# Later gates in a recurrent layer with a mixture of experts: five pairs of experts further down the program

## The chip, the cores and the metric

The kernel runs on one core of a Trainium2 chip. A core has five engines that run at the same time, each with its own queue of instructions, kept in order: TensorE (PE, matrix products; its weight loads are listed as PEld), VectorE (DVE), ScalarE (ACT), GpSimd (POOL) and SyncE (SP, which here issues the transfers). They wait for one another through semaphores. The metric is the device time of one execution in microseconds (us); lower is better. The kernel before takes 1005.94 us, the median of three runs (1005.19 to 1009.68).

## The reference

The input x has 8 batches of 1024 time steps of 256 features. In short:

```
xn = layernorm(x)
v  = xn Wv^T + bv
for each time step t:            # W starts as W0
    y_t = xn_t W^T               # the output uses W before its update
    W   = W - eta * 2/(B*D) * (y_t - v_t)^T xn_t
logits = xn Wr^T + br            # 16 experts
p      = softmax(logits), the six largest kept and divided by their sum
moe    = sum over experts e of  gate_e * (xn E_e)
out    = x + y * silu(moe)
```

All 16 expert products are computed for every token, and the gates (10 of the 16 are zero) weight them.

## The kernel before

**Tiles and slots.** Tokens go in 64 tiles of 128 rows, 16 time steps of 8 batches each. The main loop gives each tile a slot, and in a slot eight pairs of experts follow one another: `experts(i, pair)` runs six matmuls that fill one PSUM bank h with both experts' products (L539). Of each pair, DVE adds the even expert's part to a running sum (mix, L558), and for six of the odd experts ACT scales (part, L547) and POOL adds (mix, L550); the other two odd ones are DVE's as well. There are three h banks.

**The recurrence.** In its slot, a tile also has three steps that follow from W: errors_1 before pair 0, errors_2 before pair 3, update before pair 5. In errors_1 PE multiplies by W (pe), DVE forms p, and p is split into a high and a low part (p_hi on ACT, p_lo on DVE). In errors_2 PE makes the errors, ACT scales them to step_hi (L510), and DVE makes step_lo (L512) and hy (L516). In update six matmuls add to W in PSUM (wt_ps; the third is the first to use step_lo), and then W is split (wt_hi on ACT, wt_lo on DVE). Every split goes through the helper `split` (L142, L143), and most products through `accumulate` (L241).

**Ahead of W.** Five tiles ahead, other steps are put between the pairs: the load of x and the layer norm (DVE's st, mv and xn, POOL's ve and rstd, then xr, a transpose whose blocks change places by way of DRAM), the transposed tile's split (xT_two, xn_hi, xn_lo), `project` before pair 1 and `project_end` before pair 2. `project` makes the Gram matrix in gram, ACT copies a part of it to cross (L256), and DVE adds the router's bias to the logits lg. In `project_end` one matmul of PE adds cross transposed (L268), and DVE forms xx (L276) and a (L277).

**Groups.** Tiles are grouped: groups 0 to 3 have 1, 1, 2 and 4 tiles, all others (4 to 17) have 4. After a group's last projection come its gates, and, one pair later, `solve_0` (four q additions on DVE, L407); five further solve steps between later pairs invert the group's triangular matrices. The gates of groups 4 to 17 stand in the slots of tiles 6, 10, ... 58. They are DVE's work but for one exponential on ACT:

- the eight largest logits (top), the difference d to the largest, ex on ACT
- four match instructions, which mark the six largest (L366)
- s_all, chosen (L372), s_top (L375), den (L377), r_den (L378), total, acc, eps_sum, acc again, and gate (L382)

chosen, a, q, den and gate each read two tensors from SBUF; mix and xx read one from PSUM and one from SBUF.

**What sets the order.** PE and SP keep the order of the program. The other three engines' instructions are placed by a planner that runs when the program is built: it works with estimated times, takes what is ready, and goes by the program's order among those. So a step's place in the program is a wish for DVE, ACT and POOL, and the order in the built program is fixed.

Of the kernel before, what the change touches and what calls it, by code (L numbers as in the profile page):

```python
"""Layer norm, then an online-learned linear layer (one gradient step of W per time step) gated by
the silu of a top-6-of-16 mixture of linear experts, with a residual.

Tokens go in tiles of 128 rows: 16 time steps of all 8 batches, time-major. Within a tile the
recurrence is solved exactly: with A = c * X X^T restricted to strictly earlier time steps and
c = eta * 2 / (B * D), the errors of all steps are E = T (X W^T - V), T = (I + A)^-1, where W is the
weight before the tile, and W^T is then lowered by c * X^T E. The state W^T accumulates in one PSUM
bank.

U = T^T is built for a few tiles at a time from diagonal blocks of 32 rows, by Horner's rule  # L10
(I - C (I - C (I - C)), C = A^T), which merge into blocks of 64 and then 128 rows:
U_ab = -U_a C_ab U_b.

TensorE and the DMA queue keep the order given below; the other engines are scheduled around them.
All but the first tiles are transposed without TensorE: in blocks of 32 by VectorE, and the blocks
change places on their way through DRAM.

The large products split each float32 operand exactly into two float32r parts, x = hi + lo, and add
up hi*hi + hi*lo + lo*hi in float32; what is left out is below float32's own rounding.
"""  # L20

# [1 line left out]

# [11 lines left out]
PSUM = bass.MemoryType.PSUM  # L35
# [5 lines left out]
EPS = 1e-10  # L41
# [2 lines left out]
GROUP = 4  # L44
AHEAD = 5
BY_PE = 4
ON_ACT = (1, 3, 5, 7, 9, 11)


@with_exitstack  # L50
def ttt_moe_kernel(
# [13 lines left out]
    B, S, D = x.shape  # L65
# [10 lines left out]
    state = ctx.enter_context(tc.tile_pool(name="state", bufs=2))  # L76
# [11 lines left out]
    counts = [1, 1, 2]  # L88
# [22 lines left out]
    def misc(name):  # L111
        return ps_misc.tile([P, 512], F32, tag="misc", name=name)

# [1 line left out]
    raws = {}  # L115

    def fetch_expert(e):
# [19 lines left out]
    make_identity(nc, ident)  # L137
    neg_half = const.tile([P, 1], F32)
    nc.gpsimd.memset(neg_half, -0.5)
    # transposed weights: W0^T the first state, [Wv^T | router^T] one moving operand  # L140
    def split(hi, lo, src, engine=None):
        nc.scalar.copy(hi, src)  # L142
        (engine or nc.vector).tensor_sub(lo, src, hi.bitcast(F32))  # L143
# [37 lines left out]
    def at(b, size=Q):  # L181
        return slice(b * size, (b + 1) * size)

# [1 line left out]
    class Prepared:  # L185
        pass

# [2 lines left out]
    def layernorm(i):  # L190
        q = tiles[i] = Prepared()
        xt = x_tile(i)
        st = small.tile([P, nc.vector.BN_STATS_DIM], F32, tag="st", name=f"st_{i}")
        nc.vector.bn_stats(st, xt)  # L194
        mv = small.tile([P, nc.vector.BN_AGGR_DIM], F32, tag="mv", name=f"mv_{i}")
        nc.vector.bn_aggr(mv, st)  # L196
        ve = small.tile([P, 1], F32, tag="ve", name=f"ve_{i}")
        nc.gpsimd.tensor_scalar_add(ve, mv[:, 1:2], LN_EPS)  # L198
        rstd = small.tile([P, 1], F32, tag="rstd", name=f"rstd_{i}")
        nc.gpsimd.tensor_tensor(rstd, ve, neg_half, ALU.pow)  # L200
        q.xn = work.tile([P, D], F32, tag="xn", name=f"xn_{i}", bufs=3)
        nc.vector.tensor_scalar(q.xn, xt, mv[:, 0:1], rstd, ALU.subtract, ALU.mult)  # L202
        if i < BY_PE:
            return
        q.xT = work.tile([P, KD * P], F32, tag="xT", name=f"xT_{i}", bufs=3)
        # blocks of 32 are transposed in place, and change places by way of DRAM
        xr = work.tile([P, D], F32, tag="xr", name=f"xr_{i}")
        nc.vector.transpose(
            xr.rearrange("p (c k t) -> p k c t", c=NQ, k=KD),
            q.xn.rearrange("p (k c t) -> p k c t", c=NQ, k=KD),  # L210
        )
        bounce = dram.tile([NQ, Q, NQ, KD * Q], F32, tag="bounce", name=f"bounce_{i}")
        nc.sync.dma_start(out=bounce.rearrange("b d c f -> (b d) (c f)"), in_=xr)
        for c in range(NQ):
            nc.sync.dma_start(
                out=q.xT[at(c), :].rearrange("p (b f) -> p b f", b=NQ),
                in_=bounce[:, :, c, :].rearrange("b d f -> d b f"),
            )
# [15 lines left out]
        split(q.xn_hi, q.xn_lo, q.xn, nc.gpsimd)  # L234

    def accumulate(o, hi, lo, rhs_hi, rhs_lo, first=True, **kw):
        # the terms with the moving low part come last: it is ready last
        terms = [t for a, b, r in zip(hi, lo, rhs_hi) for t in ((a, r), (b, r))]
        terms += zip(hi, rhs_lo)
        for m, (a, b) in enumerate(terms):  # L240
            nc.tensor.matmul(  # L241
                o, lhsT=a, rhs=b, start=first and m == 0, stop=(m == len(terms) - 1), **kw
            )

    def project(i, g, j):
        q = tiles[i]
        # X X^T = H H^T + H L^T + (H L^T)^T
        gram = misc(f"gram_{i}")
        for k in range(KD):
            nc.tensor.matmul(  # L250
                gram[:, : 2 * P], lhsT=q.xT_hi[:, k, :],
                rhs=q.xT_two[:, k, :, :].rearrange("p n t -> p (n t)"),
                start=(k == 0), stop=(k == KD - 1), skip_group_check=True,
            )
        q.gram, q.cross = gram, work.tile([P, P], F32R, tag="cross", name=f"cross_{i}")
        nc.scalar.copy(q.cross, gram[:, P : 2 * P])  # L256
        vr = misc(f"vr_{i}")
        accumulate(
            vr[:, :NVR],
            [q.xT_hi[:, k, :] for k in range(KD)], [q.xT_lo[:, k, :] for k in range(KD)],  # L260
            [w_vr[0][:, k, :] for k in range(KD)], [w_vr[1][:, k, :] for k in range(KD)],
        )
        nc.vector.tensor_add(g.lg[:, j, :NE], vr[:, D:NVR], bias[:, D:])  # L263
        q.vr = vr
# [11 lines left out]
        nc.vector.tensor_add(xx, q.gram[:, :P], q.cross.bitcast(F32))  # L276
        nc.vector.tensor_mul(g.a[:, j, :, :], xx.unsqueeze(1).broadcast_to([P, 2, P]), masks)  # L277

# [1 line left out]
    layernorm(0)  # L280
    transpose_w()
    ident_r = const.tile([P, P], F32R)
# [6 lines left out]
    half_b = const.tile([P, D], F32)  # L289
    nc.scalar.mul(half_b, bias[:, :D], 0.5)  # L290

    # -c at strictly earlier time steps, in A's place and in A^T's
    ones = const.tile([P, P], F32)
    nc.gpsimd.memset(ones, 1.0)
    keep = const.tile([P, 2, P], F32)
# [8 lines left out]
    masks = const.tile([P, 2, P], F32)  # L304
    nc.vector.tensor_scalar_mul(masks, keep, neg_c)

    # U and the first half of T by blocks: what is never written stays zero
    u_full, t_half = [], []
    for n in range(2):
        u = const.tile([P, GROUP, P], F32, tag=f"u_{n}", name=f"u_{n}")  # L310
# [8 lines left out]
    def open_group(n, first, count):  # L319
# [14 lines left out]
        for name, t in vars(stores[m]).items():  # L334
            if name in ("t", "z2"):
                setattr(g, name, t)
            else:
                setattr(g, name, t[:, j : j + count])
        # odd tiles keep the first half of T, and what comes of it, in the upper partitions
        g.halves = []  # L340
        for odd in range(2):
            js = [n for n in range(count) if (j + n) % 2 == odd]
# [5 lines left out]
    def gates(g):  # L348
# [5 lines left out]
        def narrow(name):  # L354
            return group.tile([P, GROUP], F32, tag=name, name=f"{name}_{n}", bufs=4)[:, :c]

        # the six largest logits, the first of equal ones, are marked; two absent values fill up to eight
        lg, top, d, ex = g.lg, wide("top", 8), wide("d"), wide("ex")
        marked, chosen, gate = wide("marked", NE + 2), wide("chosen"), wide("gate", bufs=4)
        for j in range(c):  # L360
# [12 lines left out]
            chosen, marked[:, :, :NE], TAKEN, ex, op0=ALU.is_equal, op1=ALU.mult  # L373
        )
        nc.vector.tensor_reduce(s_top, chosen, AX.X, ALU.add)  # L375
        # gates p / (sum p + EPS) with p = ex / s_all, then divided by max(their sum, EPS)
        nc.vector.scalar_tensor_tensor(den, s_all, EPS, s_top, op0=ALU.mult, op1=ALU.add)  # L377
        nc.vector.reciprocal(r_den, den)  # L378
        nc.vector.tensor_mul(total, s_top, r_den)
# [7 lines left out]
            q.u_hi, q.u_lo = g.u_hi[:, j, :], g.u_lo[:, j, :]  # L387

    def step_q(g, name, rhs, out):
        """I - C rhs for the diagonal blocks."""  # L390
        c = g.count
        ps = solving(f"{name}_ps_{g.n}")
        for j in range(c):
            for b in range(P // Q):
                nc.tensor.matmul(  # L395
                    ps[at(b), j * Q : (j + 1) * Q], lhsT=g.a[at(b), j, 0, at(b)],
                    rhs=rhs[at(b), j, :], start=True, stop=True, skip_group_check=True,
                )
        nc.vector.tensor_add(
            out, ps[:, : c * Q].rearrange("p (j q) -> p j q", q=Q),  # L400
            ident_q.unsqueeze(1).broadcast_to([P, c, Q]),
        )
# [81 lines left out]

    solve = [solve_1, solve_2, solve_3, solve_4, solve_5, solve_6]

# [1 line left out]
    def errors_1(i):  # L488
        q = tiles[i]
        q.pe = ps_rec.tile([P, 2 * D], F32, tag="pe", name=f"pe_{i}")  # L490
# [70 lines left out]
                q.mix[j] = new  # L561

    def finish(i):
        # x + y silu(m) = x + (y / 2) m (1 + tanh(m / 2))
        q = tiles[i]
        xt = x_tile(i)
        m = work.tile([P, D], F32, tag="m", name=f"m_{i}")
# [9 lines left out]
            out=out[:, i * TS : (i + 1) * TS, :].rearrange("b t d -> t b d"), in_=o  # L577
        )

# [1 line left out]
    opened = {}  # L581

    def project_x(i):
        n, first, j = where[i]
        if n not in opened:
            opened[n] = open_group(n, first, counts[n])
        project(i, opened[n], j)
        if j == counts[n] - 1:
            gates(opened[n])

    def project_y(i):
        n, first, j = where[i]
# [4 lines left out]
    def solve_x(n, m):  # L597
        solve[m](opened[n])

    # what comes before each (tile, pair of experts)  # L600
    events = {}

    def put(slot, pair, what, *args):
        events.setdefault((slot, pair), []).append((what, args))

    # the first tiles have a schedule of their own: (slot, pair) as 8 * slot + pair
    chain = {
        0: (3, 9, 10), 1: (13, 16, 18), 2: (21, 23, 25), 3: (27, 29, 31), 4: (33, 38, 40),
        5: (42, 45, 47), 6: (49, 51, 55),
# [18 lines left out]
    for i in range(1, NT):  # L628
# [6 lines left out]
        put(turn // 8, turn % 8, transpose_x, i)  # L635
        put(spot // 8, spot % 8, project_x, i)
        put((spot + 1) // 8, (spot + 1) % 8, project_y, i)

    ctx.enter_context(tc.manual_schedule(engines={mybir.EngineType.PE, mybir.EngineType.SP}))

# [52 lines left out]
```

## Time and profile before

| | |
|---|---|
| time, median of three runs | 1005.94 us (1005.19 to 1009.68) |
| span of the profiled execution | 1004.7 us |
| PE busy | 977.6 us, 97% |
| DVE busy | 770.0 us, 77% |
| ACT busy, POOL busy | 436.5 us, 440.8 us |
| granted PE clock | full speed after the first twentieth of the span |
| four tiles in the steady part | 60.3 us |

The span is measured from the first to the last instruction of one execution under the profiler; the runs' times are taken without it. Times in a timeline count from the span's start. A line of the timeline gives start and length, engine, source line, operation, output and inputs, their sizes, how many instructions were merged (x2), and in brackets how long the engine had been idle and what ended that. Buffer numbers are left out of names, so that every running sum is mix and both q buffers are q.

### The profile page before, as it was taken

How to read it: one execution, taken by the hardware profiler on the slowest of the kernel's cores; microseconds unless marked ns; L12 is line 12 of the kernel's file. 1: busy time of each engine (PE TensorE's matmuls, PEld its weight loads, DVE VectorE, ACT ScalarE, POOL GpSimd, SP SyncE). 2: the span in 40 equal slices, each digit the busy share in tenths (PEclk: the TensorE clock that was granted, in tenths of full speed). 3: DMA queues.
4: the chain of work that ended last, by engine and by line, in shares of the span. 5: the costliest groups of instructions: out<-in, count | busy, mean ns of one | idle time of the engine just before them, and what ended most of it. 6: DMA issues, size and time to landing. Idle time of an engine off the chain costs nothing.

```text
span 1004.7 us, 19617 instructions
## 1 busy us (share of the span) xinstructions
PE 977.6 (97%) x6672; PEld 799.9 (80%) x6672; DVE 770.0 (77%) x2225; ACT 436.5 (43%) x1174; POOL 440.8 (44%) x677
## 2 busy tenths in 40 slices
PE   5899999999999999999999999999999999999997
PEld 4677888878888887888878888887888878888785
DVE  7888797777878777787777878778787777867665
ACT  5454444344443534435344443534435344443432
POOL 6544344444344344444444344344444444344333
PEclk8899999999999999999999999999999999999999
DMA  7021111111111111111111111011111111100000
GB/s 231 17 53 49 39 27 43 37 27 43 39 27 42 28 37 43 38 27 44 38 28 43 38 28 43 24 42 43 36 29 43 38 28 43 35 25 11 12 11 11
DMA packets 67092, 38.65 MB, mean 38 GB/s; under 512 B 38176, under 2 KB 66992, under 8 KB 66992
## 3 DMA queue, kind: packets, MB, share of 16 engines
q1 hardware_dynamic: 66992, 37.41, 13.6%
q8 instruction: 52, 0.85, 0.3%
q14 instruction: 48, 0.39, 0.1%
HBM read 21.13 MB, written 16.25 MB: 37 GB/s over the span
## 4 chain that ended last, share of the span: by engine, by line
PE 77%; DVE 14%; issue 2%; POOL 2%; DMA 2%; ACT 2%; SPq 1%; POOLq 0%; DVEq 0%; ACTq 0%
PE h L241 59%; PE pe L241 6%; PE wt_ps L241 4%; PE vr L241 3%; DVE q L407 3%; DVE mix L558 2%; DMA x<-in_L_attn_x_dram 1%; PE gram L250 1%; DVE marked L366 1%; POOL mix L550 1%; DVE st L194 1%; ACT part L547 1%; DVE o L574 1%; DVE d L362 1%; PE uq_ps L395 1%
## 5 line engine op out<-in xcount | busy, mean ns | idle before, releaser
L241 PE MATMUL h<-we,xT_two 128*128 128x512 f32 x3072 | 789.3, 402 | 4.5 <-DVE mix L558 2.5
L241 PEld LDWEIGHTS h<-we,xT_two 128*128 128x128 f32 x3072 | 554.5, 189 | 120.1 <-issue 2.7
L558 DVE SCALAR_TENSOR_TENSOR mix<-h,gate,mix 128x256 f32<-128x256 f32 x576 | 265.6, 475 | 112.0 <-PE h L241 80.1
L547 ACT ACTIVATE part<-h,gate 128x256 f32<-128x256 f32 x384 | 182.1, 474 | 293.1 <-DVE mix L558 171.4
L550 POOL TENSOR_TENSOR mix<-mix,part 128x256 f32<-128x256 f32 x256 | 188.7, 737 | 131.4 <-ACT part L547 124.0
L572 POOL TENSOR_TENSOR my<-m,hy 128x256 f32<-128x256 f32 x64 | 47.3, 739 | 159.0 <-DVE m L568 159.0
L550 POOL TENSOR_TENSOR mix<-part,part 128x256 f32<-128x256 f32 x64 | 47.9, 749 | 72.3 <-ACT part L547 72.3
L575 POOL TENSOR_TENSOR o<-o,x 128x256 f32<-128x256 f32 x63 | 46.5, 738 | 69.4 <-DVE lg L263 59.2
L194 DVE BATCH_NORM_STATS2 st<-x 128x6 f32<-128x256 f32 x64 | 27.1, 425 | 49.9 <-DMA x<-in_L_attn_x_dram 49.5
L241 PE MATMUL vr<-w_vr,xT_two 128*128 128x272 f32 x384 | 59.2, 290 | 0.0
L202 DVE TENSOR_SCALAR xn<-x,mv,rstd 128x256 f32<-128x256 f32 x64 | 49.0, 765 | 12.2 <-POOL rstd L200 11.9
L143 DVE TENSOR_TENSOR wt_lo<-wt_ps,wt_hi 128x512 fp32r<-128x512 f32 x64 | 42.9, 671 | 19.6 <-ACT wt_hi L142 19.5
L142 ACT CAST xT_two<-xT 128x256 fp32r<-128x256 f32 x60 | 24.4, 407 | 71.9 <-PE h L241 69.9
L198 POOL TENSOR_SCALAR ve<-mv 128x1 f32<-128x1 f32 x64 | 14.5, 228 | 91.2 <-DVE mv L196 56.4
L143 POOL TENSOR_TENSOR xn_lo<-xn,xn_hi 128x256 fp32r<-128x256 f32 x64 | 47.7, 746 | 14.2 <-ACT xn_hi L142 13.9
L142 ACT CAST p_hi<-p 128x256 fp32r<-128x256 f32 x64 | 26.0, 406 | 63.6 <-DVE p L498 63.5
L241 PEld LDWEIGHTS vr<-w_vr,xT_two 128*128 128x128 f32 x384 | 52.4, 191 | 0.0
L510 ACT ACTIVATE step_hi<-pe,neg_c 128x256 fp32r<-128x256 f32 x64 | 30.4, 474 | 50.5 <-PE pe L241 50.2
L241 PEld LDWEIGHTS pe<-wt_hi,xT_two 128*128 128x128 f32 x256 | 39.2, 189 | 5.9
L142 ACT CAST wt_hi<-wt_ps 128x512 fp32r<-128x512 f32 x64 | 37.2, 581 | 10.8 <-PE wt_ps L241 10.3
L241 PE MATMUL pe<-wt_hi,xT_two 128*128 128x256 f32 x256 | 40.7, 281 | 0.0
L143 DVE TENSOR_TENSOR p_lo<-p,p_hi 128x256 fp32r<-128x256 f32 x64 | 39.2, 612 | 0.9 <-ACT p_hi L142 0.4
(115 smaller groups left out, 1186.7 us busy)
## 6 DMA issues: line engine op xcount, KB each, us to landing
x<-in_L_attn_x_dram SPq DMA_DIRECT2D x64, 128.0 KB, 2.7
out_dram<-o SPq DMA_DIRECT2D x64, 128.0 KB, 2.3
bounce<-xr SPq DMA_DIRECT2D x60, 128.0 KB, 2.4
xT<-bounce SPq DMA_DIRECT2D x240, 32.0 KB, 1.8
raw<-in_L_ffn_expert_w_dram SPq DMA_DIRECT2D x16, 256.0 KB, 5.0
w_raw<-in_L_attn_Wkv_dram SPq DMA_DIRECT2D x1, 256.0 KB, 3.1
w_raw<-in_L_attn_W_dram SPq DMA_DIRECT2D x1, 256.0 KB, 5.2
bias<-in_L_attn_bkv_dram SPq DMA_DIRECT2D x1, 128.0 KB, 4.5
```

Of the source, the lines that this page charges most:

```text
L142: nc.scalar.copy(hi, src)
L143: (engine or nc.vector).tensor_sub(lo, src, hi.bitcast(F32))
L194: nc.vector.bn_stats(st, xt)
L202: nc.vector.tensor_scalar(q.xn, xt, mv[:, 0:1], rstd, ALU.subtract, ALU.mult)
L241: nc.tensor.matmul(o, lhsT=a, rhs=b, start=first and m == 0, stop=(m == len(terms) - 1), **kw)
L407: nc.vector.tensor_add(g.q1[at(b)], g.a[at(b), :, 1, at(b)], ident_q[at(b), :].unsqueeze(1).broadcast_to([Q, c, Q]),)
L510: nc.scalar.mul(q.step_hi, e, neg_c)
L547: nc.scalar.mul(part, he, gate)
L550: nc.gpsimd.tensor_add(new, q.mix[1], part)
L558: nc.vector.scalar_tensor_tensor(new, he, gate, q.mix[j], op0=ALU.mult, op1=ALU.add)
L572: nc.gpsimd.tensor_mul(my, m, q.hy)
L575: (nc.vector if i == NT - 1 else nc.gpsimd).tensor_add(o, o, xt)
```

## The change

From group 4 on (`LATE_GATES`), the gates are no longer emitted with the projection of the group's last tile, which stands before pair 1, but by an event of their own, five pairs later in the same slot: before pair 6, behind the update of W, which stands before pair 5. The instructions stay as they are. What a group's gates are used for begins with the next group's first slot, two slots later.

```diff
+LATE_GATES = 4
...
     def project_x(i):
         n, first, j = where[i]
         if n not in opened:
             opened[n] = open_group(n, first, counts[n])
         project(i, opened[n], j)
-        if j == counts[n] - 1:
+        if j == counts[n] - 1 and n < LATE_GATES:
             gates(opened[n])
 
+    def gates_x(n):
+        gates(opened[n])
...
         put(spot // 8, spot % 8, project_x, i)
         put((spot + 1) // 8, (spot + 1) % 8, project_y, i)
+        n, first, j = where[i]
+        if n >= LATE_GATES and j == counts[n] - 1:
+            put((spot + 5) // 8, (spot + 5) % 8, gates_x, n)
```

## The prediction

> **What bounds the kernel now.** I read the page's first part, then the chain that ended last, the waits of TensorE (PE), and then the timeline of single tiles.
>
> ```profile
> PE 977.6 (97%) x6672; PEld 799.9 (80%) x6672; DVE 770.0 (77%) x2225; ACT 436.5 (43%) x1174; POOL 440.8 (44%) x677
> ...
> PE 77%; DVE 14%; issue 2%; POOL 2%; DMA 2%; ACT 2%; SPq 1%; POOLq 0%; DVEq 0%; ACTq 0%
> ...
> PE wt_ps L241 <- DVE step_lo L512: 2.4, 9, 0.4
> ```
>
> PE is the bound, busy 97% of the span with an order that is fixed; only what makes PE wait, or wait longer, changes the time. In the steady part four tiles take 60.3 us. One wait recurs, once per group, in the slot (the eight pairs of one tile) where gates stand: PE's update of W waits for step_lo. In the timeline the six update matmuls, from the first to the next product's start, take 0.71 us in 48 of the 63 updates and 1.07 to 1.41 us in 12, those of tiles 10, 14, ... 54; with 0.71 taken off each, the 12 sum to 5.9 us. (Three early ones are longer for other reasons and aren't touched.) So 5.9 us is the most that a perfect cure brings.
>
> The timeline of tile 26 (group 9's gates) shows why:
>
> ```profile
> 438.50 0.48 DVE L558 SCALAR_TENSOR_TENSOR mix<-h,gate,mix 128x256 f32<-128x256 f32 x1
> 439.22 0.22 DVE L372 SCALAR_TENSOR_TENSOR chosen<-marked,ex 128x64 f32<-128x64 f32 x1
> 439.35 0.42 DVE L277 TENSOR_TENSOR a<-xx,masks 128x256 f32<-128x256 f32 x1
> 439.69 0.74 POOL L550 TENSOR_TENSOR mix<-part,part 128x256 f32<-128x256 f32 x1 [0.94 <-ACT part L547]
> 439.81 0.48 DVE L558 SCALAR_TENSOR_TENSOR mix<-h,gate,mix 128x256 f32<-128x256 f32 x1
> 440.20 0.66 DVE L407 TENSOR_TENSOR q<-a,ident_q 32x128 f32<-32x128 f32 x2
> 441.00 0.74 POOL L550 TENSOR_TENSOR mix<-mix,part 128x256 f32<-128x256 f32 x1 [0.57 <-ACT part L547]
> 441.09 1.09 DVE L407 TENSOR_TENSOR q<-a,ident_q 32x128 f32<-32x128 f32 x2
> 442.56 0.47 DVE L512 SCALAR_TENSOR_TENSOR step_lo<-pe,neg_c,step_hi 128x256 fp32r<-128x256 f32 x1
> 443.08 0.39 PE L241 MATMUL wt_ps<-step_lo,xn_hi 128*128 128x256 f32 x1 [0.37 <-DVE step_lo L512]
> ```
>
> VectorE (DVE) runs without a gap, and two of its q instructions take 1.09 us where two free ones take 0.57: the third is 0.79 instead of 0.28, because POOL's mix (441.00 to 441.74) reads SBUF at the same time and DVE ends 0.15 after it. POOL's start hangs on DVE: mix (438.50 to 438.98), ACT's part 0.09 later (0.47), POOL 0.14 after that, so 1.19 after the mix began.
>
> **What the change moves.** No instruction is added or removed, gates issue no DMA, and in the built program PE, ACT and SP keep their orders; POOL swaps two in one group (a memset of 0.10). The scheduler had placed the gates' DVE instructions among the others by readiness, and it still does. For groups 5 to 16:
>
> ```
> before: match x4, mix_2, s_all, xx, chosen, a, s_top, mix_4, q, q, den, q, q, st, step_lo
> after:  match x2, mix_2, xx, match x2, s_all, a, chosen, mix_4, q, q, q, q, s_top, st, step_lo
> before: r_den, mix_6, mv, total, mix_8, acc, eps_sum, acc, gate, xn, wt_lo, xr, mix_10
> after:  den, mix_6, mv, r_den, mix_8, total, acc, eps_sum, acc, xn, gate, wt_lo, xr, mix_10
> ```
>
> (mix_4 is the running sum after expert 4; hy follows step_lo in both.) By lengths alone this is nothing or a small gain: only den, 0.19 from start to start, passes step_lo, 12 x 0.19 = 2.3 us. But the order decides who meets POOL. I walk tile 26 with the spacings of its own rows.
>
> *Step 1, chosen.* Two matches fewer (0.146 each) let mix_2 start at 438.21; its h is there (PE's next work began at 437.64). xx 438.60, matches and s_all to 439.10, a at 439.23, chosen at 439.56. ACT's part comes 0.29 sooner and POOL's first mix at 438.21 + 1.19 = 439.40, inside a. So chosen, which has two inputs in SBUF, finds POOL ahead of it. Who goes first? In the trace, wherever POOL's tensor operation began during one such DVE instruction and another followed at once, the second waited for POOL: den then q, and gate then xn (0.40 free, 0.81 here), 26 of 26 times from 139 us on, once with POOL's start only 0.02 ahead. Here it is 0.16 ahead.
>
> How long does POOL hold out? The Trainium skill, "SBUF — State Buffer", section "Who interferes with whom", says that the second to issue fully blocks until the first has finished. By that rule POOL would wait for the end of a at 439.65 and run 0.74, to 440.39. The rows say less: POOL's mix that starts 0.24 into another tile's a, with 0.19 left, is recorded as 0.785 instead of 0.74, so for 0.25 left I estimate 0.10 more: to 440.24. I take the row; the rule would add 0.15 per group, 1.8 us in all. A blocked chosen ended 0.08 after POOL (0.73 us in tile 6's slot), here 440.32; mix_4 starts 0.08 before that end, 440.24, against 439.81.
>
> *Step 2, step_lo.* From mix_4, the q start at +0.39, +0.68, +0.98 and +1.28; POOL's next mix is again at +1.19. The third q now gets through; the fourth is blocked until POOL's end (0.74) plus 0.15, +2.07, or 442.31. Then s_top (start +0.03), st (+0.13), step_lo (+0.34) at 442.81, done 443.28 (mix_4 + 3.04) against 443.03: **0.25 later**, and PE's wait is longer, not shorter. x's load was issued at 438.43 and lands in 2.7 us, so st doesn't wait.
>
> *Step 3, gate.* All that follows is 0.25 later. The new place of gate is the dearer part:
>
> ```profile
> 444.74 0.23 DVE L382 TENSOR_TENSOR gate<-chosen,acc 128x64 f32<-128x64 f32 x1
> 444.83 0.73 POOL L550 TENSOR_TENSOR mix<-mix,part 128x256 f32<-128x256 f32 x1
> 444.90 0.81 DVE L202 TENSOR_SCALAR xn<-x,mv,rstd 128x256 f32<-128x256 f32 x1
> 445.52 0.78 POOL L143 TENSOR_TENSOR xn_lo<-xn,xn_hi 128x256 fp32r<-128x256 f32 x1
> 445.63 0.68 DVE L143 TENSOR_TENSOR wt_lo<-wt_ps,wt_hi 128x512 fp32r<-128x512 f32 x1
> ```
>
> Before, gate slips in ahead of POOL's mix, in time that xn would wait for rstd anyway. After it, gate is issued 0.08 before xn's end, 445.71 + 0.25 - 0.08 = 445.88, and xn_lo has started at 445.77 (0.04 before POOL's mix ends), 0.11 ahead. gate waits to xn_lo's end 446.55 + 0.08, and wt_lo starts at 446.55 instead of 445.63: **0.92 later** (0.25, 0.14 for gate's own place, 0.53 blocked).
>
> *Step 4, what is late next.* The chain from there has no slack: xr, mix_10, ACT part, POOL mix, three mix of DVE (448.51), xT_two, p, ACT p_hi, th, four u, four t, and then ACT's copy cross, each starting when the one before lets it. That copy feeds a matmul of PE:
>
> ```profile
> 453.38 0.27 ACT L256 CAST cross<-gram 128x128 fp32r<-128x128 f32 x1
> ...
> 454.00 0.33 PE L268 MATMUL gram<-ident_r,cross 128*128 128x128 f32 x1
> ```
>
> Here PE comes 0.35 after cross, in each of these 12 slots (0.33 to 0.35); in the other slots 1.4 or more. With cross 0.92 later and 0.05 to release PE, PE is 0.92 + 0.05 - 0.35 = **0.62 later**; this holds step 2's 0.25, since both are on one path. Other consumers keep their cover: wt_lo is needed at 448.92 (2.6 us after its end, 1.7 left), xT_two was done about 0.8 before PE's gram loads its weights (0.1 left, PE being 0.25 later itself), p_lo is needed over 2 us later. If the 0.1 is gone, too, some 0.1 per group comes on top.
>
> *Sum.* 12 x 0.62 = 7.4 us. Group 17's gates (tile 58) have no xn and no later gram; its step_lo was just in time (done at +0.08 from the update's start), and by step 2 it comes at +0.49: 0.4. Group 4's stand where step_lo is 3 us early: 0. In all **+7.8 us**: span 1004.7 + 7.8 = 1012.5. The runs' median stands 1.2 above that span, so 1005.94 + 7.8 = **1013.7 us**.
>
> **Rivals.** (a) *gate isn't blocked*, because xn lets go later or gate comes sooner: step 2 alone, 12 x 0.25 + 0.4 = +3.4, 1009.3. Against it: the order of starts in step 3 follows from one POOL end. (b) *chosen isn't blocked, gate is*: mix_4 at 439.69, step_lo at 439.69 + 3.04 = 442.73, 0.30 earlier; gate's chain 0.67 - 0.30 = 0.37 later, PE 0.37 + 0.05 - 0.35 = 0.07 later; with group 17 about +1, 1007. (c) *The other side*: neither is blocked, since DVE's next instruction keeps the port while POOL queues. Then step_lo is 0.30 earlier: -3.6 us, 1002.3; if the fourth q also gets past POOL, all of 5.9 goes, 1000.1. It decides at chosen: if that lasts 0.22 us and not 0.75, this case is on. For it: den's shift is real; against: the 26 encounters. (d) *The move does nothing*: the scheduler shifts the gates by only a few places, so no visible effect, 1005.9. That needs POOL's encounters to stay as they are, and POOL's start is tied to mix_2, which moves by 0.29. (e) *Worse*: xT_two's 0.1 is gone, or delays add up as by the skill's rule: +10, 1016.
>
> **How the numbers follow.** Forecast 0.60, (a) 0.10, (b) 0.08, (c) 0.11, (d) 0.03, (e) 0.08. The likeliest alone is 1012 to 1015.5 (0.1 us per group either way, and the runs' own spread). For 8 in 10, I cut most of (c) and the top of (e): 1003 to 1016.5. A measurement here tells 0.5% (5 us) from no change: slower by more is the forecast, (e) and a little of (a), less the forecast's low tail, 0.66; within is (a), (b), (d) and most of (c), 0.29; faster only the full form of (c), 0.05.
>
> **What would show it.** Of the changed kernel: chosen about 0.75 us and gate about 0.75 in groups 5 to 16 (0.22 and 0.23 before); the third q free, the fourth near 0.8; updates of tiles 10 to 54 about 0.25 longer; a new PE wait at the matmul that adds cross, 0.3 to 0.4 each; four tiles in 60.9 us instead of 60.3. A short chosen, a short gate, or cross still ahead of PE would prove the step named wrong.

## The result and the profile after

The changed kernel takes 1009.78 us (median of 18 runs, 1007.6 to 1013.06) where the kernel before, run on the same chip in turn with it, takes 1007.43 (18 runs, 1004.89 to 1009.93). The ratio is 1.0028 with an interval of 1.0019 to 1.0038: about 2.8 us slower, which is inside the 0.5% that was called no change, and little more than a third of the 7.8 us that were forecast. The profiled execution spans 1008.0 us (1004.7 before).

The page of the changed kernel, first part and the chain that ended last:

```profile
PE 976.7 (97%) x6672; PEld 798.4 (79%) x6672; DVE 772.7 (77%) x2225; ACT 434.2 (43%) x1174; POOL 445.6 (44%) x677
...
PE 71%; DVE 15%; ACT 4%; issue 3%; POOL 3%; DMA 2%; SPq 1%; POOLq 0%; DVEq 0%; ACTq 0%
```

PE's work is what it was; DVE is busy 2.7 us longer with the same 2225 instructions, and POOL 4.8 us with its 677. The instructions became longer, not more: DVE and POOL hold each other up, as the timeline below shows place by place. The waits of TensorE (engine, line, what it waited for: us in total, times, longest):

```profile
PE gram L269 <- ACT cross L257: 3.9, 12, 0.3
...
PE wt_ps L242 <- DVE step_lo L513: 0.6, 2, 0.3
```

The first line is new. The second stood at 2.4 us, 9 times, before: that wait became shorter, where the forecast had made it longer.

To see what each place is worth I set every matmul of one trace against the same matmul of the other, and summed by place how much later PE gets there. (For these sums every single step is taken, also those too short to be listed as a wait.) From before to after:

| place | PE later, us |
|---|---|
| up to 60 us (loads and set-up, no gates of groups 4 to 17) | +0.23 |
| 60 to 160 us (group 4's gates, from 136 us on) | +0.32 |
| the 12 updates of tiles 10 to 54, at step_lo | -1.91 (their excess over 0.709 us falls from 5.88 to 3.96) |
| the 12 matmuls that add cross | +4.76 (0.39 to 0.41 each) |
| all, with small rest | +3.34 |

The first row says how far one profiled span may be trusted: up to 60 us, PE in the kernels of the experiments came from 1.45 us earlier to 1.91 us later than in the kernel before, with nothing changed there. So single spans aren't compared to less than some 2 us below; places are.

All line numbers of the changed kernel are one higher. Tile 26 in its timeline, in the rows that stand for those shown before:

```profile
439.87 0.47 DVE L559 SCALAR_TENSOR_TENSOR mix<-h,gate,mix 128x256 f32<-128x256 f32 x1
...
440.88 0.41 DVE L278 TENSOR_TENSOR a<-xx,masks 128x256 f32<-128x256 f32 x1
...
441.06 0.97 POOL L551 TENSOR_TENSOR mix<-part,part 128x256 f32<-128x256 f32 x1
441.21 0.22 DVE L373 SCALAR_TENSOR_TENSOR chosen<-marked,ex 128x64 f32<-128x64 f32 x1
...
441.35 0.48 DVE L559 SCALAR_TENSOR_TENSOR mix<-h,gate,mix 128x256 f32<-128x256 f32 x1
441.74 1.77 DVE L408 TENSOR_TENSOR q<-a,ident_q 32x128 f32<-32x128 f32 x4
...
444.01 0.47 DVE L513 SCALAR_TENSOR_TENSOR step_lo<-pe,neg_c,step_hi 128x256 fp32r<-128x256 f32 x1
...
446.36 0.81 DVE L203 TENSOR_SCALAR xn<-x,mv,rstd 128x256 f32<-128x256 f32 x1
...
446.98 0.78 POOL L144 TENSOR_TENSOR xn_lo<-xn,xn_hi 128x256 fp32r<-128x256 f32 x1
...
447.09 0.75 DVE L383 TENSOR_TENSOR gate<-chosen,acc 128x64 f32<-128x64 f32 x1
...
447.76 0.68 DVE L144 TENSOR_TENSOR wt_lo<-wt_ps,wt_hi 128x512 fp32r<-128x512 f32 x1
...
455.52 0.27 ACT L257 CAST cross<-gram 128x128 fp32r<-128x128 f32 x1
...
455.84 0.33 PE L269 MATMUL gram<-ident_r,cross 128*128 128x128 f32 x1 [0.32 <-ACT cross L257]
```

Three things are to be seen. chosen comes 0.15 behind the start of POOL's mix, as forecast, but it takes 0.22 us, and it is POOL that waits: 0.97 instead of 0.74. gate, behind xn, takes 0.75 instead of 0.23, ending 0.08 after POOL's xn_lo, as forecast. And cross ends only 0.05 before the matmul that reads it, with PE idle 0.32 before that: the cover of 0.35 is gone.

### The profile page after: what moved, and what is told of

Same layout as the page of the kernel before. It is cut to its first block, busy times and chain, and to the rows that moved or that the text cites. A ratio compares the mean times of both kernels' runs of the same rounds, so it can differ in the third digit from the quotient of the medians.

```text
span 1008.0 us, 19617 instructions
## 1 busy us (share of the span) xinstructions
PE 976.7 (97%) x6672; PEld 798.4 (79%) x6672; DVE 772.7 (77%) x2225; ACT 434.2 (43%) x1174; POOL 445.6 (44%) x677
## 4 chain that ended last, share of the span: by engine, by line
PE 71%; DVE 15%; ACT 4%; issue 3%; POOL 3%; DMA 2%; SPq 1%; POOLq 0%; DVEq 0%; ACTq 0%
PE h L242 55%; PE pe L242 5%; PE wt_ps L242 4%; PE vr L242 3%; DVE mix L559 3%; DVE q L408 2%; DMA x<-in_L_attn_x_dram 2%; POOL mix L551 2%; PE gram L251 1%; ACT part L548 1%; ACT t L426 1%; ACT u L423 1%; DVE marked L367 1%; PE gram L269 1%; PE z_ps L467 1%
## 5 line engine op out<-in xcount | busy, mean ns | idle before, releaser
L551 POOL TENSOR_TENSOR mix<-part,part 128x256 f32<-128x256 f32 x64 | 50.4, 787 | 63.9 <-ACT part L548 63.3
```

Source lines behind the costliest of these rows:

```text
L551: nc.gpsimd.tensor_add(new, q.mix[1], part)
```

## The experiments

All times are beside the kernel before on the same chip. "behind" is a helper in these kernels that fixes the order of two instructions on one engine and nothing else.

| kernel | us, before beside it | ratio | step_lo: excess of 12 updates, us | PE later at 12 crosses, us | wt_lo starts / cross ends / gram matmul, us after the update's start |
|---|---|---|---|---|---|
| before | | 1 | 5.88 | 0 | 3.16 / 11.17 / 11.52 |
| after | 1009.78, 1007.43 | 1.0028 (1.0019 to 1.0038) | 3.96 | 4.76 | 3.67 / 11.69 / 11.74 |
| e1 after, gate alone in the next slot | 1004.59, 1006.61 | 0.9977 (0.9967 to 0.9987) | 3.84 | 0 | 2.98 / 10.99 / 11.33 |
| e2 before, gate alone in the next slot | 1006.99, 1006.61 | one run | 6.45 | 0 | 3.17 / 11.19 / 11.53 |
| e4 after, xn_lo left out | 1003.46, 1006.61 | one run | 4.09 | 0 | 3.27 / 11.29 / 11.35 |
| e5 after, s_all between a and chosen | 1010.51, 1007.56 | one run | 1.75 | 6.82 | 3.67 / 11.68 / 11.73 |
| e6 after, gates behind hy | 1001.25, 1007.56 | 0.9945 (0.9924 to 0.9966) | 0.0 | 0 | 2.95 / 10.42 / 11.05 |
| e3 gates whole in the next slot | 1001.59, 1006.61 | 0.9947 (0.9930 to 0.9963) | 0.0 | 0 | 2.44 / 10.44 / 11.05 |
| e9 before, 0.68 us of DVE behind wt_lo | 1009.94, 1007.56 | 1.0031 (1.0017 to 1.0045) | 6.12 | 3.71 | 3.22 / 11.83 / 11.88 |
| e8 before, 0.29 us of DVE behind wt_lo | 1009.01, 1007.56 | one run | 6.40 | 0 | 3.18 / 11.41 / 11.53 |
| e7 after, group 4 in its old place | 1007.49, 1006.40 | one run | 3.38 | 4.79 | 3.58 / 11.60 / 11.65 |

The last column holds medians over the 12 slots. How to read it: without any wait PE needs 11.05 us from the update's start to the gram matmul (e3, e6); a late step_lo adds its 0.15 to 0.5; and in no row is PE there before the end of cross plus 0.05. The excess at step_lo scatters by some 0.6 us between traces in which nothing ahead of it was changed (5.88 before, 6.45 in e2, 6.40 in e8).

**e1 and e2: the gate product by itself.** The forecast's third and fourth steps say that gate, held by POOL ahead of wt_lo, is what costs. So take it alone out of that place:

```diff
-        nc.vector.tensor_mul(gate, chosen, acc.unsqueeze(2).broadcast_to([P, c, NE]))
+        g.gate_args = gate, chosen, acc.unsqueeze(2).broadcast_to([P, c, NE])
+        if n < 5:
+            nc.vector.tensor_mul(*g.gate_args)
...
+    def gate_x(n):
+        behind(nc.vector.tensor_mul(*opened[n].gate_args), last_a[0])
...
+        if m >= 5 and j == counts[m] - 1:
+            put((spot + 10) // 8, (spot + 10) % 8, gate_x, m)
```

e1 is the changed kernel with this edit; last_a is the newest a.

> The changed kernel, but the product gate alone (groups 5 to 17) goes to the next slot, behind a there; all else keeps its order. Theory (gate, put directly behind xn, is held by POOL's xn_lo and makes wt_lo and the chain up to cross late): wt_lo starts at xn's end again, about 0.67 us sooner after the update's start, the 12 waits of PE for cross (0.39 us each, with the restart) are gone, and the 12 waits for step_lo stay as in the changed kernel (4.0 us in all): 4.7 us less than the changed kernel, 1.5 us less than the kernel before, ratio about 0.9985. Rival (the waits for cross come from the other instructions that moved, total and acc): the waits stay, ratio 1.003.

Measured 0.9977 (0.9967 to 0.9987): all of the loss is gone, and the rest of the change is a gain. In the timeline of e1:

```profile
444.70 0.78 POOL L153 TENSOR_TENSOR xn_lo<-xn,xn_hi 128x256 fp32r<-128x256 f32 x1
...
444.81 0.68 DVE L153 TENSOR_TENSOR wt_lo<-wt_ps,wt_hi 128x512 fp32r<-128x512 f32 x1
...
452.56 0.27 ACT L266 CAST cross<-gram 128x128 fp32r<-128x128 f32 x1
...
453.16 0.33 PE L278 MATMUL gram<-ident_r,cross 128*128 128x128 f32 x1
...
453.85 0.42 DVE L287 TENSOR_TENSOR a<-xx,masks 128x256 f32<-128x256 f32 x1
...
454.09 0.79 POOL L564 TENSOR_TENSOR mix<-part,part 128x256 f32<-128x256 f32 x1 [1.23 <-ACT part L561]
...
454.19 0.76 DVE L609 TENSOR_TENSOR gate<-chosen,acc 128x64 f32<-128x64 f32 x1
```

wt_lo follows xn directly, cross is 0.33 ahead of PE again, and PE doesn't wait. gate is held up by POOL in its new place just as long (0.76 in 12 of 12, behind a), where nobody waits for it. The same edit made to the kernel before (e2) should do nothing, since gate there stood in time that xn would have waited anyway.

> The kernel before, but the product gate alone (groups 5 to 17) goes to the next slot, behind a there. Theory (in the kernel before gate costs nothing, as it lies in the time in which xn waits for rstd): wt_lo and cross as before, PE's 12 waits for step_lo as before (5.9 us): no change, ratio 1.000. Rival (gate is on the path there too): wt_lo 0.14 us sooner or more, and 1 to 2 us less.

It did nothing that can be told: wt_lo, cross and gram are within 0.02 us of the kernel before. Place, not length, makes the gate product dear.

**e4: what holds gate up.** Here the low part of xn is left out (set to zero) for the W update of every fourth tile from 16, so POOL has a short memset where xn_lo was:

```diff
-        split(q.xn_hi, q.xn_lo, q.xn, nc.gpsimd)
+        if i % GROUP == 0 and i >= 16:
+            nc.scalar.copy(q.xn_hi, q.xn)
+            nc.gpsimd.memset(q.xn_lo.bitcast(F32), 0.0)
+        else:
+            split(q.xn_hi, q.xn_lo, q.xn, nc.gpsimd)
```

> The changed kernel, but POOL's xn_lo of every fourth tile (16, 20, ...) is replaced by a POOL memset of zeros, which reads nothing; so the low part of those tiles' xn is left out of their update of W. The order on DVE is that of the changed kernel. Theory (the two-input gate is held while POOL reads SBUF): gate takes 0.23 us instead of 0.75, wt_lo comes 0.5 us sooner, and PE waits for cross little or not at all (cross 0.1 us before PE needs it): about 4 us less than the changed kernel. Rival (gate is slow because of what it waits for, acc or xn, not because of POOL): gate stays at 0.75 us, and the time at the changed kernel's.

The wait for cross went as the theory said, but by another way. The timeline of e4, tile 26:

```profile
442.87 0.31 POOL L237 MEMSET xn_lo<- 128x256 f32 x1
442.96 0.41 DVE L203 TENSOR_SCALAR xn<-x,mv,rstd 128x256 f32<-128x256 f32 x1
...
443.15 1.63 POOL L555 TENSOR_TENSOR mix<-mix,part 128x256 f32<-128x256 f32 x2
...
443.29 0.75 DVE L387 TENSOR_TENSOR gate<-chosen,acc 128x64 f32<-128x64 f32 x1
...
443.96 0.68 DVE L144 TENSOR_TENSOR wt_lo<-wt_ps,wt_hi 128x512 fp32r<-128x512 f32 x1
```

The memset was early and over quickly, POOL's next mix came forward in xn_lo's stead, and gate stood behind that: still 0.75. What became free was xn (0.41 instead of 0.81 in these 12 slots), because POOL's mix now begins 0.19 after xn and not 0.07 before it. So the edit removed one hold-up of 0.4 and not the one aimed at; cross then ends at 11.29, and PE, still 0.34 late at step_lo, arrives just in time. It shows gate held by another tensor operation that POOL had begun, and isn't proof for xn_lo in particular; that gate's place is what costs rests on e1.

**e5: who goes first at chosen.** In the changed kernel chosen follows a directly, issued 0.08 before a ends. Here s_all, a sum over one tensor, is put between them:

```diff
-        nc.vector.tensor_reduce(s_all, ex, AX.X, ALU.add)
-        nc.vector.scalar_tensor_tensor(
+        s_all_of = nc.vector.tensor_reduce(s_all, ex, AX.X, ALU.add)
+        chosen_of = nc.vector.scalar_tensor_tensor(
...
+        if n > 4:
+            behind(s_all_of, last_a[0])
+            behind(chosen_of, s_all_of)
```

> The changed kernel with s_all put between a and chosen (groups 5 to 17); the scheduler then puts the four q ahead of mix_4, so the time says little and the look is at chosen alone. Theory (DVE keeps the port when its next two-input instruction is issued before the last has ended; a gap, or an instruction with one input, lets waiting POOL in): chosen is held and takes 0.6 to 0.75 us, POOL's mix 0.8 to 0.85 us. Rival (DVE goes first whenever it asks within some 0.3 us of POOL): chosen 0.22 us, POOL's mix 0.97 us or more.

```profile
440.93 0.42 DVE L287 TENSOR_TENSOR a<-xx,masks 128x256 f32<-128x256 f32 x1
...
441.24 0.74 POOL L565 TENSOR_TENSOR mix<-part,part 128x256 f32<-128x256 f32 x1
441.26 0.21 DVE L383 TENSOR_REDUCE s_all<-ex 128x4 f32<-128x64 f32 x1
...
441.39 0.66 DVE L384 SCALAR_TENSOR_TENSOR chosen<-marked,ex 128x64 f32<-128x64 f32 x1
...
441.98 1.17 DVE L422 TENSOR_TENSOR q<-a,ident_q 32x128 f32<-32x128 f32 x4
```

This is the chosen of the forecast: 0.66 us in 13 of 13, ending 0.08 after POOL. In both kernels POOL's mix begins 0.15 before chosen (0.149 to 0.158 after, 0.152 to 0.162 here). With a directly ahead, chosen goes first and POOL takes 0.97; with s_all between, POOL goes first and takes its 0.74. My theory had expected POOL at 0.80 to 0.85 here. Its 0.74 shows the second thing that differs: POOL begins only 0.11 before the end of a, instead of 0.23, and isn't held up by a at all. So this run doesn't tell whether s_all lets POOL in, or the earlier end of a.

The theory itself, that DVE keeps POOL out when its next two-input instruction is issued before the last has ended, doesn't hold in general. The rows of e1 above answer it: there gate stands directly behind a, issued 0.08 before its end just as chosen is in the changed kernel, and POOL goes first (gate 0.76, POOL 0.79; 12 of 12, and 12 of 12 again in e2). POOL begins 0.19 before the end of a there and 0.11 before gate; at chosen it is 0.23 and 0.15. Whether these hundredths decide or the two kinds of instruction isn't separated by any run.

And yet the update doesn't suffer. The four q now come ahead of mix_4 and take 1.17 instead of 1.77, because POOL's next mix, whose start hangs on DVE's mix_4, no longer falls on them; step_lo's excess drops to 1.75. So a blocked chosen doesn't by itself make step_lo late, if the order behind it differs. PE gained nothing from it: gram stands at 11.73 after the update's start, as in the changed kernel (11.74), because cross is unmoved at 11.68. What PE saves at step_lo it waits at cross.

**e6 and e3: another place for the whole of the gates.** In the changed kernel the planner put the larger part of the gates, up to s_top, ahead of step_lo anyway. e6 keeps all of them behind hy of the same slot:

```diff
-LATE_GATES = 4
+LATE_GATES = 5
...
-        gates(opened[n])
+        with tc.issue_after(last_hy[0].ins):
+            gates(opened[n])
```

> The changed kernel, with all of DVE's gate instructions of groups 5 to 17 held behind hy of the same slot, so that they really stand behind step_lo; group 4's as in the kernel before. Theory (the slot has two limits: step_lo, and the chain from wt_lo to cross, which has 0.3 us to spare): the 12 waits for step_lo are gone (-5.9 us), but chosen or gate, held by POOL, and the other gates' instructions make wt_lo and cross late, so that PE waits for cross for 0.4 to 0.9 us in each of 12 slots: between 1 us less and 5 us more than the kernel before, ratio 0.999 to 1.005. Rival (only step_lo matters): as with the gates in the next slot, ratio 0.9945.

Here my theory missed and the rival held: 0.9945 (0.9924 to 0.9966). I had expected the gates' work between step_lo and wt_lo to make cross late. The timeline of e6, tile 26, whose update starts at 440.26:

```profile
442.47 0.72 POOL L153 TENSOR_TENSOR xn_lo<-xn,xn_hi 128x256 fp32r<-128x256 f32 x1
442.52 0.75 DVE L384 SCALAR_TENSOR_TENSOR chosen<-marked,ex 128x64 f32<-128x64 f32 x1
...
443.20 0.68 DVE L153 TENSOR_TENSOR wt_lo<-wt_ps,wt_hi 128x512 fp32r<-128x512 f32 x1
...
450.40 0.27 ACT L266 CAST cross<-gram 128x128 fp32r<-128x128 f32 x1
...
451.31 0.33 PE L278 MATMUL gram<-ident_r,cross 128*128 128x128 f32 x1
```

chosen now pays the hold-up that gate paid (0.75 in 11 of 13), right ahead of wt_lo. But DVE, which has none of the gates' work before step_lo, finishes step_lo 0.45 before the update starts, instead of 0.63 after it (444.48 against 443.85 in the changed kernel), 1.1 us more in hand; and s_top to gate come only after wt_lo, gate itself 6.55 us after the update's start, free of POOL (0.22). So wt_lo is at 2.95, and cross ends 0.50 to 0.64 ahead of PE's matmul in 11 of the 12 slots (1.21 in the last). What I had left out is that a DVE which is ahead at step_lo is ahead at wt_lo, too.

e3 puts the gates of groups 5 to 17 whole into the next slot, behind its a:

```diff
-LATE_GATES = 4
+LATE_GATES = 5
...
-        gates(opened[n])
+        with tc.issue_after(last_a[0].ins):
+            gates(opened[n])
...
-            put((spot + 5) // 8, (spot + 5) % 8, gates_x, n)
+            put((spot + 10) // 8, (spot + 10) % 8, gates_x, n)
```

> All gates of groups 5 to 17 are issued in the next slot, behind a there; group 4's stand where they stood before. Theory (the 12 waits for step_lo are there because the gates delay it on DVE, and the next slot has DVE time to spare): no wait for step_lo and none for cross, 5.9 us less than the kernel before, ratio 0.994. Rival (the gates only carry their delay with them: in the next slot they push wt_lo, cross or step_lo late as well): new waits of PE in the slots of tiles 11, 15, ... 55, ratio 0.998 to 1.003.

Measured 0.9947 (0.9930 to 0.9963), with both waits gone. The waits of TensorE in e3, complete:

```profile
PE wtr L161 <- DMA w_raw<-in_L_attn_Wkv_dram: 5.3, 1, 5.3
PE q_ps L407 <- DVE q L419: 3.6, 5, 1.0
PE gram L260 <- DVE xT_two L153: 3.4, 1, 3.4
PE h L251 <- ACT part L559: 2.6, 2, 1.9
PE h L251 <- DVE mix L570: 2.5, 1, 2.5
PE z_ps L478 <- ACT t L471: 0.7, 1, 0.7
PE y_ps L463 <- ACT z L453: 0.2, 1, 0.2
```

Neither step_lo nor cross is in it. e3 and e6 both beat the kernel before by about 0.54%; they can't be told from each other.

**e9 and e8: the cover at cross, measured in the kernel before.** An idle sum on DVE, over 520 or 150 elements, is put behind wt_lo in the 12 slots:

```diff
+        lo_of = split(hi.rearrange("p k e -> p (k e)"), lo.rearrange("p k e -> p (k e)"), wt_ps)
+        if 11 <= i <= 55 and i % 4 == 3:
+            extra[0] = nc.vector.tensor_reduce(
+                extra_out, w_raw.rearrange("p c d -> p (c d)")[:, :520], AX.X, ALU.add
+            )
+            behind(extra[0], lo_of)
...
+                    if e == 10 and 10 <= i <= 54 and i % 4 == 2:
+                        behind(mixed, extra[0])
```

The last two lines keep mix_10, DVE's next running sum on the way to cross, behind the idle sum.

> The kernel before, with one idle instruction of DVE (a sum over 520 elements of one SBUF tensor, about 0.6 us) behind wt_lo in the 12 slots. Theory (from wt_lo to cross there is no slack but the 0.35 us that PE comes after cross, less 0.05 for its release): PE waits for cross 0.30 us in each, 12 x 0.30 = 3.6 us more, ratio 1.0036; the waits for step_lo stay. Rival (the chain has slack elsewhere, at POOL or ACT): PE waits less or not at all, ratio 1.000 to 1.001.

> As the run with the long idle instruction, but a sum over 150 elements, about 0.22 us. Theory: inside the 0.30 us of cover, so cross is 0.22 us nearer to PE's need (about 0.13 us ahead of it) and PE's time is that of the kernel before. Rival (any delay there costs PE its length): 2.6 us more.

The long one takes 0.68 and moves the end of cross by 0.66; PE is late there by 3.71 us in sum, 0.31 each (forecast 0.30), with this line in its waits:

```profile
PE gram L284 <- ACT cross L272: 2.9, 12, 0.3
```

The short one takes 0.29 and moves cross by 0.24: it ends 0.12 to 0.15 before PE comes, and no wait for cross is in the list. Its span, 1007.0, looks 2.3 us longer than before, but 1.91 of that lie in the first 60 us and 0.37 in the next 100, where nothing was changed; from 160 us on PE is within 0.1 us of the kernel before. So the cover of 0.35 is real, with 0.05 to release PE: a delay of 0.24 is free, and of one of 0.66 all beyond 0.30 comes through (PE's matmul is 0.36 later after the update's start).

**e7: group 4's share.** The late place from group 5 on only (`LATE_GATES = 5`, one character).

> The changed kernel with the late place from group 5 on only: group 4's gates stand where they did before. The forecast costed group 4's move at nothing; the trace of the changed kernel shows PE 0.32 to 0.39 us later within that group's slot (143 to 148 us of the span, mostly at the products that use wt_lo). Theory (the move of group 4's gates did it): that step is gone, PE within 0.05 us there of the kernel before, and everything else as in the changed kernel: 12 waits of PE for cross of 0.3 us, 12 updates with 4.0 us of excess in sum, span about 0.3 under 1008.0. Rival (it drifts there from the start-up's timing, whatever the gates do): 0.3 us late there, as in the changed kernel.

The steps at the products with wt_lo in group 4's slot (+0.28 and +0.10) aren't in this trace; the largest step of PE between 60 and 160 us is -0.11. So the move of group 4's gates makes these steps: they are in all four traces that have it (after, e1, e4, e5: 0.37 to 0.40 in sum), and in none of the others. But that isn't its cost. In the same four traces PE comes 0.26 to 0.51 us earlier at a product of the experts 4 us ahead of these steps (in the others at most 0.11 earlier or later). Over the whole slot, 142 to 148 us, PE ends from 0.12 us earlier to 0.15 later in the four, and from 0.11 earlier to 0.12 later in the others. Of the +0.32 in the table, 0.18 is a step at 133 us, ahead of group 4's gates; e8, whose gates stand in their old place, has such a step, too. A cost of group 4's move can't be told from nothing. The 12 waits for cross are all there (4.79 us).

## Why the prediction was right or wrong

**Step 1 (chosen) failed.** chosen was said to find POOL ahead, to wait for it and to take 0.75, with mix_4 0.43 later. POOL was ahead, by 0.15, and yet chosen took 0.22 in 13 of 13; the one that waited was POOL. The "26 of 26" were encounters of other kinds: den then q, where DVE issued the next instruction only after the one before had ended (0.03 us later), and gate then xn, where it was issued 0.07 before that end, but reads one tensor. None was a two-input instruction with another two-input one issued before its end. Of that kind the runs have both outcomes: chosen behind a goes first, gate behind a (e1, e2) waits. So that chosen goes first is shown, and why is open. By the order of issue, which the Trainium skill has decide ("SBUF — State Buffer", "Who interferes with whom"), chosen would have been the one that waits. That the lock is exclusive, as that section also says, agrees with the traces, if POOL's start is counted 0.14 later than recorded: POOL's instruction grows by 0.05 where DVE had 0.19 left (a, before), by 0.23 where it had 0.37 (a and chosen, after), and by 0.38 where it had 0.52 (u_lo, a difference of two tensors in SBUF, after).

**Step 2 (step_lo) fell with it.** Not 0.25 later, but 0.16 earlier on average (1.91 / 12; 0.08 in tile 26, where the first q was held, too: 0.43 for the forecast's 0.28). The fourth q was blocked, as forecast (0.74).

**Step 3 (gate) held**, to the hundredth: 0.75 in 12 of 12, 0.08 after the end of POOL's xn_lo. In tile 26 wt_lo starts 3.92 after the update's start, against 3.31: these 0.61 are about the 0.14 for gate's place and the 0.53 of hold-up (0.67), less what step_lo gained (0.08 in that tile). e1 takes this away, and with it the loss.

**Step 4 (what is late next) held.** The chain has no slack: in tile 26 cross moved by 0.61, as wt_lo did. The new wait stands at the matmul that was named, in all 12 slots; e9 and e8 measure the cover as forecast (0.35 with 0.05 to release).

**Sum.** The term that was wrong is step 2's +0.25, which rests on step 1. With the measured -0.16 in its place, the forecast's other terms give (0.67 - 0.16) + 0.05 - 0.35 = 0.21 per group; measured 0.24 ((4.76 - 1.91) / 12). That is 2.9 us for the twelve groups instead of 7.4; four tiles take 60.6 us, where the forecast had 60.9. Group 17 was to add 0.4 by step 2 and added nothing (its update takes 0.709, 0.713 before). Group 4 was costed at nothing, and no cost can be told; the reason given, an early step_lo, left out the products with wt_lo, where PE comes 0.38 later, and the gain of 0.29 just ahead of them.

**The rivals.** (b) was the mechanism: chosen free, gate blocked. It came to +1 because it put step_lo 0.30 earlier. In tile 26 it was 0.08: DVE was already 0.13 later against PE when the gates began, so that mix_4 stood where it had stood before, and POOL's mix, held up by chosen, ran on into the first q; from mix_4's start to step_lo's end it is 3.13, where 3.04 was forecast. (c) named the right test, chosen at 0.22, and then supposed that gate would go free as well: POOL's start was 0.11 to 0.15 ahead at both places, and the outcomes were opposite. (a) needed a free gate, (d) no new encounters, and (e) an additional loss; none is seen.

The forecast put 0.60 on one chain of which each later step rested on the first. Its answer to who goes first at chosen was taken from encounters that looked alike in their starts, and not in the kind of DVE's two instructions and how they followed one another. The measured time lies inside its range of 8 in 10, but by way of (b), which had 0.08.

## What to carry to other kernels

A wait that is cured on one engine is worth only what the next chain to the same engine leaves: here PE saved 0.16 per group at step_lo and lost 0.40 at cross, and e5 saved 4.1 us at step_lo for nothing. Before an instruction is moved, look at how far each later consumer is covered (0.35 us here, in one slot of four), and place work that can wait, like these gates, behind the chain instead of in front of it: the same instructions in the next slot (e3) made the kernel 0.5% faster instead of 0.3% slower. Counting encounters in a trace is evidence only for encounters of the same shape, with the same two instructions and the same spacing: chosen and gate, each issued 0.08 before the end of a, fared differently.

## What was not expected of the hardware

- The later start can go first. chosen issued 0.08 before the end of a, POOL's mix begun 0.15 before chosen: chosen 0.22, POOL 0.97 (13 of 13). With s_all between, and POOL's start the same 0.15 ahead of chosen: chosen 0.66, POOL 0.74 (13 of 13).
- Neither the spacing nor the instruction ahead decides it alone. gate is issued 0.08 before the end of xn (after, e4) or of a (e1, e2), POOL begins 0.11 to 0.14 ahead of it, and POOL goes first each time (0.75 to 0.76 in 12 of 12). What sets chosen behind a apart is open.
- xn, which reads one tensor and two columns of scalars, is held up by POOL, too: 0.81 where POOL's mix began 0.07 before it, 0.41 where it began 0.19 after it (e4).
- The held-up DVE instruction ended 0.08 after POOL's in each of these places (chosen in e5 0.080 to 0.086, gate 0.080 to 0.085).
- A held-up POOL instruction grows by what DVE's two-input instructions had left at its start, less 0.14 (0.19, 0.37 and 0.52 left: 0.05, 0.23 and 0.38 more).
